# Reordering the first loads of a split-float32 matmul kernel, with one more engine allowed for part of the weights

## The chip, the cores and the metric

The kernel runs on one core of a Trainium2 chip. The metric is device time in microseconds (us). Before the change the median of three runs is 107.62 us (107.62 to 107.70). The core's engines are named as in the profile: PE is TensorE (matmuls; PEld its weight loads), DVE is VectorE, ACT is ScalarE, POOL is GpSimd, SP is SyncE, which here only issues DMAs. A "q" behind a name (SPq, ACTq) is that engine's instruction sequencer, where DMA issues show.

## The reference

With `x` of shape (4, 1024, 512) and one condition vector of 256 elements per batch row:

```python
hidden = concat([cond, cond], -1)                       # (4, 512)
x_mean = mean(x, axis=1, keepdims=True)                 # (4, 1, 512)
fused = concat([x, x_mean * ones, hidden * ones], -1)   # (4, 1024, 1536)
return x + relu(einsum('bld,do->blo', fused, W) + b)    # W: (1536, 512)
```

Everything is float32. `W` has three blocks of 512 rows: the first multiplies `x`, the second the mean, the third the condition. Only the first block needs a large matmul; the other two give one bias vector per batch row.

## The kernel before

**Tiles.** The 4096 rows of `x` are 32 tiles of 128 rows; tile `t` is row `r = t // 8`, `k = t % 8`. A tile needs 128x512 outputs over a contraction of 512, which is cut into J = 4 slices of 128. Each operand is split into a high part rounded to the matmul's float32 format and a low remainder, so that each slice takes three matmuls: high by high, high of x by low of W, low of x by high of W. That makes 12 matmuls with 512 columns per tile.

**Preparing x.** Tiles are grouped in units: tiles 0 and 1 alone, tiles 2-3, 4-5 and 6-7 in pairs, then fours. The first four units (`TURN_PE`) are turned by PE transposes straight from the loaded tile (line 388); later units are loaded a second time in another arrangement (`z`, line 284) and turned on DVE (line 390). A turned piece lies in PSUM, in one of two buffers, or for a few pieces in SBUF. ACT copies it to `hi` (line 415), DVE or POOL subtracts to get `lo` (line 431). For the two single tiles DVE also adds up columns for the mean (`sum`, line 424). A turn may start when the piece two before it has been split (and, for a single tile, added up), because it takes over that buffer.

**Preparing W.** The first block of W comes in two halves of 512 KB, slices 0 and 1 by `load_w(e, 0)`, slices 2 and 3 by `load_w(e, 2)` (line 293). Each slice then has `w_hi` (line 358 on ACT or 359 on DVE) and `w_lo` (line 361, DVE only).

**Finishing.** When a tile's 12 matmuls (line 594) are done, its PSUM bank is read out with or without bias (lines 607, 612), relu follows on ACT (617), `x` is added on POOL (620), and the tile is stored (632). The last four tiles are finished on DVE alone (612, 625), the very last one in two halves. A row's bias comes from the sums, the mean block and the condition block of W and is spread over 128 partitions by two matmuls (line 520).

**The order.** The program fixes, for every engine, one instruction order ahead of time. Each operation is added to a `Plan` with the engines that may run it and their costs, what it depends on, and a due time. `latest_starts` turns due times into latest starts; `simulate` then repeatedly takes the operations that could start first (within 0.1 us of the first on the same engine), gives the turn to the one with the smallest latest start, and puts an operation with several possible engines where it would end first. `run` repeats this 1500 times with random shifts of the latest starts above 12 us and keeps the best order by the planner's own costs. Loads at the head are not planned: the loop at line 296 issues them in the order of its list, and the second entry is the time at which the planner takes them to be there. On the chip the engines keep the planned order and wait on semaphores.

**The head.** SP issues, in this order: tile 0 of x (256 KB), half 0 of W, tile 1 of x, half 1 of W, tiles 2-3 of x, tiles 4-5 of x (512 KB each), then the first slice of the mean block. All go through one DMA queue. PE runs nine warm-up matmuls on a constant (line 235), turns tile 0 (`turn 0`), transposes the condition and runs `N_FILL = 3` more matmuls on ones (`fill`, lines 397 and 401), turns tile 1 (`turn 1`), and starts the products. Products of tiles 0 and 1 are planned matmul by matmul, as `part(t, j, n)`, n = 0 for high by high, 1 for low of W, 2 for low of x. `turn 2` is the first slice of tiles 2-3.

Of the kernel before, what the change touches and what calls it, by code (L numbers as in the profile page):

```python
# [153 lines left out]
def kernel(  # L154
# [22 lines left out]
    nc = tc.nc  # L177
# [12 lines left out]
    N_FIRST = 1  # L190
# [5 lines left out]
    NEVER = 1000.0  # L196
# [3 lines left out]
    KEEP = (0, 1, 2, 3, 4, 8, 9, 10, 16, 17)  # L200
    LO_POOL = {(r, u, j) for r in (1, 2) for u in (0, 1) for j in (1, 3)} | {(0, 4, 3)}

    N_FILL = 3

    const = ctx.enter_context(tc.tile_pool(name="const", bufs=1))
    xpool = ctx.enter_context(tc.tile_pool(name="xpool", bufs=X_BUFS))
# [10 lines left out]
    plan = Plan(["pe", "dve", "act", "pool", "sp", "aq"])  # L217
# [5 lines left out]
    Wv = W.rearrange("(s p j) o -> s p j o", p=P, j=J)  # L223
# [40 lines left out]
    w_x = xpool.tile([P, J, D], F32, tag="x", name="w_x")  # L264
    w_mean = const.tile([P, J, D], F32, name="w_mean")

    def load_x(e, g, i=0, n=G):
        r, k = divmod(g * G, NK)
        if not i:
            xs[g] = xpool.tile([P, G, D], F32, tag="x", name=f"x{g}")  # L270
        e.dma_start(out=xs[g][:, i : i + n], in_=xv[r, :, k + i : k + i + n, :])  # L271
# [17 lines left out]
    SP = 0.72  # L289
    SPZ2 = 1.85  # L290
    SPZ = 1.3
    def load_w(e, j):
        e.dma_start(out=w_x[:, j : j + 2, :], in_=Wv[0, :, j : j + 2])  # L293

    nc.scalar.dma_start(out=c_sb, in_=cond)
    for key, at, e, load in (
        (("x", 0, 0), 4.4, nc.sync, lambda e: load_x(e, 0, 0, 1)),
        (("w", 0), 6.1, nc.sync, lambda e: load_w(e, 0)),
        (("x", 0, 1), 6.8, nc.sync, lambda e: load_x(e, 0, 1, 1)),
        (("w", 2), 8.1, nc.sync, lambda e: load_w(e, 2)),  # L300
        (("x", 0, 2), 9.4, nc.sync, lambda e: load_x(e, 0, 2, 2)),
        (("x", 1, 0), 10.7, nc.sync, lambda e: load_x(e, 1, 0, 2)),
    ):
        load(e)
        plan.done[key] = (at - plan.HANDOVER, 0.0, "sp")
    w_cond = xpool.tile([P, 2, KH, D], F32, tag="x", name="w_cond")

    def load_cond():
        nc.sync.dma_start(
            out=w_cond, in_=W[2 * D : 3 * D].rearrange("(s h p) o -> p s h o", p=P, h=KH)  # L310
        )
# [3 lines left out]
    def load_mean(j, n):  # L315
        nc.sync.dma_start(out=w_mean[:, j : j + n, :], in_=Wv[1, :, j : j + n])

    load_mean(0, N_FIRST) if N_FIRST else None
    plan.free["sp"] = 8.6 + SP * N_FIRST
    plan.add("cond", {"sp": 4 * SP}, [], 13, lambda e: load_cond(), later=2.5)  # L320
    plan.add("w_mean", {"sp": (J - N_FIRST) * SP}, ["cond"], 14,
             lambda e: load_mean(N_FIRST, J - N_FIRST), later=2.5)
# [31 lines left out]
    w_hi = const.tile([P, J, D], F32R, name="w_hi")  # L354
    w_lo = const.tile([P, J, D], F32R, name="w_lo")
    for j in range(J):
        plan.add(("w_hi", j), {"act": 0.62, "dve": 0.45}, [("w", j // 2 * 2)], NEVER, lambda e, j=j: (
            nc.scalar.activation(w_hi[:, j, :], w_x[:, j, :], AF.Copy) if e == "act" else
            nc.vector.tensor_copy(w_hi[:, j, :], w_x[:, j, :])))
        plan.add(("w_lo", j), {"dve": 0.69}, [("w_hi", j)], NEVER,  # L360
                 lambda e, j=j: nc_of[e].tensor_tensor(
                     w_lo[:, j, :], w_x[:, j, :], w_hi[:, j, :].bitcast(F32), ALU.subtract))

# [31 lines left out]
    def fill():  # L395
        for h in range(KH):
            nc.tensor.transpose(
                pw[:, h * B : (h + 1) * B], c_sb[:, h * P : (h + 1) * P], ident[:B, :B]
            )
        for _ in range(N_FILL):  # L400
            nc.tensor.matmul(
                pw[:, KH * B :], lhsT=warm[:, :P], rhs=warm[:, KH * B :], start=True, stop=True
            )

    plan.add(("b",), {"act": 0.25}, [("w_hi", J - 1)], FIRST + 4, lambda e: nc.scalar.dma_start(
        out=b_sb[0:1, :], in_=b.rearrange("(o d) -> o d", o=1)), later=3.0)
    plan.add(("fill",), {"pe": 0.22 * N_FILL + 0.2}, [("turn", 0)], 5.6, lambda e: fill())

    def split_hi(c):
        u, js = pieces[c]  # L410
# [24 lines left out]
    for c, (u, js) in enumerate(pieces):  # L435
        r, k0, n = units[u]
# [11 lines left out]
        w = n * len(js)  # L448
# [273 lines left out]
```

## Time and profile before

| What | Value |
|---|---|
| Median of three runs | 107.62 us |
| The profiled execution | 107.12 us |
| Its span, first to last instruction | 105.3 us |
| PE busy | 100.3 us, 95% of the span |
| DVE / ACT / POOL busy | 78.1 / 58.0 / 73.0 us |
| 512-column product matmuls (line 594) | 372, and 24 with 256 columns |
| Granted PE clock | full in every slice |

A span counts from the first to the last instruction; 1.8 us of the profiled execution lie outside it. Matmuls overlap in the records: one takes about 0.40 us from start to end, while the next starts 0.23 us after it, so that start-to-start times, not durations, say what PE does per matmul. Busy shares are averages; which wait matters is read from the order of events.

### The profile page before, as it was taken

How to read it: one execution, taken by the hardware profiler on the slowest of the kernel's cores; microseconds unless marked ns; L12 is line 12 of the kernel's file. 1: busy time of each engine (PE TensorE's matmuls, PEld its weight loads, DVE VectorE, ACT ScalarE, POOL GpSimd, SP SyncE). 2: the span in 40 equal slices, each digit the busy share in tenths (PEclk: the TensorE clock that was granted, in tenths of full speed). 3: DMA queues.
4: the chain of work that ended last, by engine and by line, in shares of the span. 5: the costliest groups of instructions: out<-in, count | busy, mean ns of one | idle time of the engine just before them, and what ended most of it. 6: DMA issues, size and time to landing. Idle time of an engine off the chain costs nothing.

```text
span 105.3 us, 1466 instructions
## 1 busy us (share of the span) xinstructions
PE 100.3 (95%) x444; PEld 79.1 (75%) x444; DVE 78.1 (74%) x119; ACT 58.0 (55%) x137; POOL 73.0 (69%) x66
## 2 busy tenths in 40 slices
PE   7969999999999999999999999999999999999980
PEld 2446878888878887888788878887888788878870
DVE  0079664769999978699859999798899964295460
ACT  5046566986799770976279773461988122290000
POOL 6000009652999999989959999996899999069200
PEclk9999999999999999999999999999999999999999
DMA  2979999999999999999999999999959755207832
GB/s 71 282 259 380 319 334 297 225 200 197 199 199 199 243 216 353 286 212 265 281 319 388 285 217 341 385 385 346 334 174 348 304 226 218 104 0 275 313 139 70
DMA packets 23905, 26.83 MB, mean 255 GB/s; under 512 B 1237, under 2 KB 14809, under 8 KB 23898
## 3 DMA queue, kind: packets, MB, share of 16 engines
q1 hardware_dynamic: 23888, 26.74, 91.3%
q8 instruction: 3, 0.05, 0.2%
q14 instruction: 4, 0.03, 0.1%
q10 hardware_dynamic: 10, 0.01, 0.0%
HBM read 18.36 MB, written 8.39 MB: 254 GB/s over the span
## 4 chain that ended last, share of the span: by engine, by line
PE 87%; DMA 7%; SPq 2%; DVE 0%; issue 0%
PE po_None L594 81%; DMA x<-in_x_dram 7%; PE po L594 3%; PE xT L388 2%; PE pb L520 2%; SPq L293 1%; SPq L271 1%; DVE o L625 0%; PE po L589 0%
## 5 line engine op out<-in xcount | busy, mean ns | idle before, releaser
L594 PE MATMUL po_None<-w_hi,hi 128*128 128x512 f32 x124 | 49.5, 399 | 0.0
L594 PE MATMUL po_None<-w_hi,lo 128*128 128x512 f32 x124 | 49.5, 399 | 0.0
L594 PE MATMUL po_None<-w_lo,hi 128*128 128x512 f32 x124 | 49.0, 397 | 0.0
L620 POOL TENSOR_TENSOR o<-o,x 128x512 f32<-128x512 f32 x28 | 35.5, 1292 | 4.2 <-ACT o L617 4.1
L390 DVE STREAM_TRANSPOSE xT<-z 128x512 f32<-128x512 f32 (+1 forms) x28 | 28.3, 1040 | 1.6 <-POOL lo L431 1.3
L594 PEld LDWEIGHTS po_None<-w_hi,hi 128*128 128x128 f32 x124 | 23.4, 189 | 5.5 <-ACT hi L415 0.2
L594 PEld LDWEIGHTS po_None<-w_lo,hi 128*128 128x128 f32 x124 | 23.4, 189 | 5.4
L594 PEld LDWEIGHTS po_None<-w_hi,lo 128*128 128x128 f32 x124 | 23.4, 189 | 5.4
L415 ACT ACTIVATE hi<-xT 128x512 fp32r<-128x512 f32 (+1 forms) x38 | 20.2, 534 | 10.1 <-PE xT L388 7.1
L431 DVE TENSOR_TENSOR lo<-xT,hi 128x512 fp32r<-128x512 f32 (+1 forms) x29 | 16.8, 581 | 8.9 <-ACT hi L415 8.6
L617 ACT ACTIVATE o<-o 128x512 f32<-128x512 f32 x28 | 16.6, 626 | 5.0 <-DVE o L612 2.7
L612 DVE TENSOR_TENSOR o<-po_None,bias 128x512 f32<-128x512 f32 x18 | 11.6, 680 | 6.7 <-issue 3.4
L612 POOL TENSOR_TENSOR o<-o,bias 128x512 f32<-128x512 f32 x10 | 13.0, 1306 | 2.6 <-issue 1.3
L495 DVE SCALAR_TENSOR_TENSOR acc<-w_mean,tot,acc 128x512 f32<-128x512 f32 x15 | 11.2, 749 | 1.3 <-ACT acc L489 0.9
L478 POOL TENSOR_TENSOR wc<-w_cond 128x512 f32<-128x512 f32 x2 | 2.5, 1294 | 13.6 <-DMA w_cond<-in_L_cond_W_dram 13.6
L431 POOL TENSOR_TENSOR lo<-xT,hi 128x512 fp32r<-128x512 f32 (+1 forms) x9 | 11.2, 1239 | 0.9 <-ACT hi L415 0.9
L607 ACT ACTIVATE o<-po_None 128x512 f32<-128x512 f32 x10 | 5.8, 592 | 7.8 <-PE po_None L594 7.8
L415 ACT ACTIVATION_READ_ACCUMULATOR hi<-xT 128x1 f32 x36 | 7.0, 195 | 0.0
L506 POOL TENSOR_TENSOR cond<-bL,term 128x512 f32<-128x512 f32 x4 | 5.2, 1304 | 2.1 <-ACT term L501 2.1
L388 PEld LDWEIGHTS xT<-ident,x 128*128 128x128 f32 x24 | 4.2, 203 | 3.3 <-DMA x<-in_x_dram 1.4
L526 ACT ACTIVATE bias<-pb 128x512 f32<-128x512 f32 x4 | 2.4, 598 | 7.7 <-PE pb L520 7.7
L501 ACT ACTIVATE term<-wc,cT 128x512 f32<-128x512 f32 x8 | 5.6, 722 | 1.0 <-POOL cond L506 1.0
(51 smaller groups left out, 58.1 us busy)
## 6 DMA issues: line engine op xcount, KB each, us to landing
out_dram<-o SPq DMA_DIRECT2D x31, 256.0 KB, 3.6
z<-in_x_dram SPq DMA_DIRECT2D x24, 256.0 KB, 8.2
x<-in_x_dram SPq DMA_DIRECT2D x6, 1024.0 KB, 8.4
x<-in_x_dram SPq DMA_DIRECT2D x3, 512.0 KB, 8.3
w_x<-in_L_cond_W_dram SPq DMA_DIRECT2D x2, 512.0 KB, 5.8
w_cond<-in_L_cond_W_dram SPq DMA_DIRECT2D x1, 1024.0 KB, 9.5
w_mean<-in_L_cond_W_dram SPq DMA_DIRECT2D x1, 768.0 KB, 9.0
x<-in_x_dram SPq DMA_DIRECT2D x2, 256.0 KB, 4.1
```

The lines of the kernel that those rows point to most:

```text
L388: nc.tensor.transpose(v[:, (m * n + i) * P : (m * n + i + 1) * P], x_t[:, j], ident)
L390: nc.vector.transpose(v[:, : n * P].rearrange("p (n t) -> p n t", t=Q), zs[u].rearrange("p n (a j) -> p n j a", j=J)[:, : n * NQ, js[0], :],)
L415: nc.scalar.activation(hi[c][:, :m], xT[c][:, :m], AF.Copy, accum_out=sums[:, r, js[0], s : s + 1] if len(js) == 1 else None,)
L431: nc_of[e].tensor_tensor(lo[c][:, :m], xT[c][:, :m], hi[c][:, :m].bitcast(F32), ALU.subtract)
L495: nc.vector.scalar_tensor_tensor(acc[r], w_mean[:, j, :], totals[r][:, j : j + 1], acc[r], ALU.mult, ALU.add)
L501: nc.scalar.activation(terms[r, k], wc[:, k], AF.Copy, scale=cT[:, k, r : r + 1])
L506: nc.gpsimd.tensor_tensor(conds[r], conds[r] if k else bL, terms[r, k], ALU.add)
L594: nc.tensor.matmul(pos[key][:, :w], lhsT=v[p][:, c], rhs=m[:, j, d], start=(not h and todo[key] == 3 * J), stop=(todo[key] == 1),)
L607: nc.scalar.activation(o_tile(t), pos[t], AF.Copy)
L612: nc_of[e].tensor_tensor(v if t >= ALONE else o_tile(t), v, biases[t // NK][:, d], ALU.add)
L617: nc.scalar.activation(outs[t], outs[t], AF.Relu)
L620: nc.gpsimd.tensor_tensor(outs[t], outs[t], x_tile(t), ALU.add)
```

## The change

Tile 1 of x is issued right behind tile 0, ahead of both halves of W; W's halves and the rest keep their order. The times that the planner assumes for the head's loads are changed with it. `fill` now follows `turn 1` instead of `turn 0` and has four matmuls on ones instead of three. `w_lo` may be planned on POOL as well as on DVE. `load_w` gets the number of slices as an argument; both calls still load two. The planner's SP is free 0.3 us later. The whole order is searched anew with these inputs.

```diff
-    N_FILL = 3
+    N_FILL = 4
...
-    def load_w(e, j):
-        e.dma_start(out=w_x[:, j : j + 2, :], in_=Wv[0, :, j : j + 2])
+    def load_w(e, j, n):
+        e.dma_start(out=w_x[:, j : j + n, :], in_=Wv[0, :, j : j + n])
...
         (("x", 0, 0), 4.4, nc.sync, lambda e: load_x(e, 0, 0, 1)),
-        (("w", 0), 6.1, nc.sync, lambda e: load_w(e, 0)),
-        (("x", 0, 1), 6.8, nc.sync, lambda e: load_x(e, 0, 1, 1)),
-        (("w", 2), 8.1, nc.sync, lambda e: load_w(e, 2)),
-        (("x", 0, 2), 9.4, nc.sync, lambda e: load_x(e, 0, 2, 2)),
-        (("x", 1, 0), 10.7, nc.sync, lambda e: load_x(e, 1, 0, 2)),
+        (("x", 0, 1), 5.0, nc.sync, lambda e: load_x(e, 0, 1, 1)),
+        (("w", 0), 6.7, nc.sync, lambda e: load_w(e, 0, 2)),
+        (("w", 2), 8.3, nc.sync, lambda e: load_w(e, 2, 2)),
+        (("x", 0, 2), 9.6, nc.sync, lambda e: load_x(e, 0, 2, 2)),
+        (("x", 1, 0), 10.9, nc.sync, lambda e: load_x(e, 1, 0, 2)),
...
-    plan.free["sp"] = 8.6 + SP * N_FIRST
+    plan.free["sp"] = 8.9 + SP * N_FIRST
...
-        plan.add(("w_hi", j), {"act": 0.62, "dve": 0.45}, [("w", j // 2 * 2)], NEVER, lambda e, j=j: (
+        plan.add(("w_hi", j), {"act": 0.62, "dve": 0.45}, [("w", {0: 0, 1: 0, 2: 2, 3: 2}[j])], NEVER, lambda e, j=j: (
...
-        plan.add(("w_lo", j), {"dve": 0.69}, [("w_hi", j)], NEVER,
+        plan.add(("w_lo", j), {"dve": 0.69, "pool": 1.33}, [("w_hi", j)], NEVER,
...
-    plan.add(("fill",), {"pe": 0.22 * N_FILL + 0.2}, [("turn", 0)], 5.6, lambda e: fill())
+    plan.add(("fill",), {"pe": 0.22 * N_FILL + 0.2}, [("turn", 1)], 5.8, lambda e: fill())
```

## The prediction

> **What bounds the kernel now.** I read the chain that ended last first, in order of time.
>
> ```profile
> 1.63 0.42 SPq L271
> 2.10 0.43 SPq L293
> 2.53 0.04 issue
> 2.57 7.38 DMA x<-in_x_dram
> 9.95 0.14 issue
> 10.09 0.48 PE xT L388 x2
> 10.57 0.94 PE po_None L594 x4
> ```
>
> Up to 9.95 us the end is set by one transfer, tiles 2-3 of x, issued at 2.57 and landed at 9.95; from turn 2 at 10.09 it is PE to the end. The busy times of the stretches 7 to 10.09, 10.09 to 102.25 and 102.25 to the end (columns: length, then PE, PEld, DVE, ACT, POOL, clock, DMA share, GB/s) say how firm that is:
>
> ```profile
> 7.00:10.09 3.09, 2.85 (x13) 2.03 (x14) 2.94 (x5) 1.75 (x3) 0.00 (x0) 1.00 0.97 360
> 10.09:102.25 92.16, 92.15 (x413) 74.81 (x413) 73.50 (x110) 53.50 (x130) 71.36 (x57) 1.00 0.95 262
> 102.25:105.30 3.05, 0.00 (x0) 0.00 (x0) 0.42 (x1) 0.00 (x0) 0.00 (x0) 1.00 0.26 89
> ```
>
> PE is busy 92.15 of 92.16 us behind turn 2, at full clock. The change removes no matmul, so time can only be won ahead of 10.09, or by having more of PE's work done by then. Last, the PE timeline of the head:
>
> ```profile
> 4.51 0.63 PE L388 MATMUL xT<-ident,x 128*128 128x128 f32 x4
> 5.28 0.82 PE L401 MATMUL pw<-const-bfloat16-1.0 128*128 128x504 bf16 x3
> 6.98 0.75 PE L388 MATMUL xT<-ident,x 128*128 128x128 f32 x4 [0.89 <-DMA x<-in_x_dram]
> 7.49 0.48 PE L594 MATMUL po_None<-w_hi,hi 128*128 128x512 f32 x1
> ...
> 9.45 0.40 PE L594 MATMUL po_None<-w_hi,lo 128*128 128x512 f32 x1
> 10.09 0.48 PE L388 MATMUL xT<-ident,x 128*128 128x128 f32 x2 [0.24 <-DMA x<-in_x_dram]
> ```
>
> Turn 1 waits for tile 1 until 6.98, then nine products run (7.49 to the slot that ends at 9.68), then PE waits for tiles 2-3. The question is therefore: how many products stand ahead of turn 2 after the change, when are they done, and when do tiles 2-3 land?
>
> **Part 1, the loads.** x1 is issued at about 1.16 instead of 1.63, half 0 of W at 1.6 instead of 1.16. Landings of half 0 and half 1, and what started on half 0:
>
> ```profile
> DMA to landing us min/median/max: 5.1/5.8/6.5
> 6.29 0.63 ACT L358 ACTIVATE w_hi<-w_x 128x512 fp32r<-128x512 f32 x1 [0.52 <-DMA w_x<-in_L_cond_W_dram]
> ```
>
> So half 0 landed at 1.16 + 5.1 = 6.26, half 1 at 2.10 + 6.5 = 8.6; tile 0 at 0.73 + 2.9 = 3.6 (the shortest landing of x). The trace shows the landings in the order of issue. Half 0 in third place has the same 1,024 KB up to its end as x1 had, so I put it where x1 was: 6.93, 0.05 before turn 1 started. Bounds from the two W rows: 5.1 us from its new issue gives 6.7, 6.5 us gives 8.1; the equal bytes decide for 6.93. x1, between 3.6 and 6.26, I put at 4.9, halfway for half the bytes. Half 1 and tiles 2-3 keep place, issue and bytes ahead: 8.6 and 9.95. Behind them SP's next issues wait for landings (w_cond started at 6.29, when half 0 landed, a z load at 6.95, when x1 did); these two waits now hang on x1 and on half 0, at 4.9 and 6.93. w_cond can be issued over 1 us earlier, but stands behind the same transfers in the queue, and its reader on POOL started only at 15.84. Cost nothing, gain nothing.
>
> **Part 2, turn 1 and fill.** PE runs turn 0 from 4.51 to 5.07, turn 1 (0.47 = 7.45 - 6.98) to 5.54, the two condition transposes (5.28 - 5.07 = 0.21), then four matmuls on ones at some 0.21 each: done at 6.6. What hides this is the wait for W. Without that cover, if x1 landed after about 6.1, turn 1 and fill (1.5 us together) would stand ahead of the first product. 0.47 us of transposes leave the stretch behind 6.98.
>
> **Part 3, splitting.** ACT: hi of tile 0 at 5.17, of tile 1 next, 0.60 each, done by 6.4; w_hi of slice 0 from 6.98 to 7.61 (0.63 of line 358). DVE: lo of tile 0 from 5.80, lo of tile 1 from 6.40 to 7.09 (back to back they start 0.60 apart: 9.01, 9.61, 10.21), then w_hi of slice 1 at 7.00 to 7.50 (0.42), w_lo of slice 0 from 7.64 to 8.33, both sums to 9.5, w_lo of slice 2 to 10.2. Following the planner's rule by hand with its new costs, two of the four w_lo, of slices 1 and 3, end first on POOL. (The same walk through the old inputs gives exactly the old trace's order of DVE and of the nine products; I use it for order alone.) POOL has no instruction between 2.3 and 15.84, and takes 1.30 for such a subtraction (line 431, 128x512, on POOL):
>
> ```profile
> L431 POOL TENSOR_TENSOR lo<-xT,hi 128x512 fp32r<-128x512 f32 x8 | 10.4, 1302 | 0.0
> L361 DVE TENSOR_TENSOR w_lo<-w_x,w_hi 128x512 fp32r<-128x512 f32 x4 | 2.7, 684 | 0.1
> ```
>
> So w_lo of slice 1 runs from 7.55 to 8.85, of slice 3 from about 9.85 to 11.15. DVE loses 2 x 0.68 of work in a stretch where nothing waits for it. The Trainium skill, "GPSIMD Engine Reference", section 1, warns that GpSimd shares its SBUF interfaces with VectorE and contends with VectorE instructions that have two SBUF inputs; w_lo of slice 0 on DVE is one, beside w_lo of slice 1 on POOL, and the trace of before has no such pair. If POOL stood still for that one, by the page slice 1 would come 0.68 later, at 9.53, just when it is needed below, and the sum would stay the same.
>
> **Part 4, the products.** The walk gives for PE: high by high and low of x for slice 0 of tiles 0 and 1 (four that need w_hi only), high by high of slice 1, the two with w_lo of slice 0, low of x of slice 1, and the one with w_lo of slice 1. Then turn 2. Again nine. First at 7.66 (w_hi 7.61 plus the 0.05 that PEld took behind hi at 8.37 to 8.42), then 0.234 apart: the sixth at 8.83 needs w_lo of 8.33, the ninth at 9.53 that of 8.85, and the slot ends at 9.77. Turn 2 also needs the first sum, done by 8.9. So PE comes to turn 2 at 9.77 and waits for tiles 2-3: 10.09 as before. The idle of 0.4 ahead of turn 2 becomes 0.3, the gain of 0.47 from turn 1 is eaten by the 0.17 later first product and by that wait.
>
> **Sum.** At 10.09 both orders have done both turns, fill and nine products; 15 parts of tiles 0 and 1 and all else are left, 92.16 us. Loads: 0. Fill's fourth matmul: 0 (under the wait for W). POOL: 0. Turn 2: 10.09 - 10.09 = 0. Span 105.3, its execution 107.12 with the 1.8 around it; the median of the runs shown stands 0.5 above that, and I add the same nothing to it: 107.62, rounded to **107.6 us**. A kernel like this can be told from no change by about 0.2%, 0.2 us.
>
> **Rivals.** (a) Faster: PE's slack of 0.32 at turn 2 turns into time. For it: if tiles 2-3 land earlier, PE follows down to 9.77, and if the order puts a tenth product ahead of turn 2, that fits too (0.23). The queue ran unevenly: 232 GB/s between 4 and 7 us against 360 from 7 to 10.09, so the order may ease that. Against: bytes ahead of tiles 2-3 are the same. Time 107.62 - 0.3 = 107.3; with half 0 at 6.7 as well, 0.55, 107.07.
> (b) Slower: half 0 of W is late. Place: the first product, which now hangs on the third load alone. It decides from 6.93 + 0.32 = 7.25 on; past that, each us is paid. At the upper bound of 8.1 PE comes to turn 2 at 9.77 + 1.17 = 10.94: 0.85 later, 108.5; with 7.7, 108.1. For it: W's rows spread from 5.1 to 6.5. Against: equal bytes.
> (c) Slower: the re-searched order, from 15 us on, lets PE wait once for a split piece. Price: one hi of 0.60 on ACT, as when a lo waits for its hi; 108.2, less if some of it was covered. For it: 92 us without a gap leave no way to improve, only to lose. Against: DVE at 74 of 92 us, POOL at 71, ACT at 54 have room.
> (d) The planner doesn't use POOL: then w_lo of slices 1 and 3 come later on DVE (9.7 and 11.5 or so), one other part takes the ninth place, and the time stays 107.6; this counts within the forecast.
>
> **How the numbers follow.** No change 0.40 (107.6, its own range 107.4 to 107.8), (a) 0.24, (b) 0.18, (c) 0.18. Faster 0.24, same 0.40, slower 0.36. The range reaches to 107.2 at the fast side (0.4 of the 0.55 that (a) could give) and to 108.4 at the slow one, just under the bound of (b); about 2 in 10 lie outside.
>
> **What would show it.** In the new profile: turn 1 behind turn 0 at about 5.1 and the first product near 7.7 (parts 1 to 3); two subtractions of line 361 on POOL; nine products, then a wait for x ahead of the third turn at 10.1 (part 4); PE busy without a gap from there to 102.25. I am wrong if tiles 2-3 land far from 9.95, if PE comes to turn 2 after them, if more than nine products stand ahead of it, or if PE waits after 15 us.

## The result, and the profile after

| | Before | After |
|---|---|---|
| Median (six runs each, side by side) | 107.66 us | 109.37 us |
| Lowest to highest | 107.62 to 109.29 | 108.28 to 111.27 |
| Ratio, 95% interval | | 1.0133 (1.0086 to 1.0180) |
| Profiled execution, span | 107.12, 105.3 us | 108.28, 106.5 us |
| End of the last product | 102.25 us | 103.43 us |

The change makes the kernel 1.3% slower; 107.6 was forecast. The ratios here leave out runs more than 1.5% above the fastest of their kernel, so they are not quite the quotients of the medians. The profiled execution of after is the quickest of its six, so what its trace shows is the smaller part of the loss.

The chain that ended last, in order of time (start, length, what), is no longer DMA up to turn 2 and PE from there:

```profile
1.64 5.72 DMA w_x<-in_L_cond_W_dram
7.37 0.02 issue
7.39 0.64 ACT w_hi L358
8.03 0.02 issue
8.05 1.69 DVE w_lo L361
9.74 0.60 DVE sums L424
10.34 1.22 DVE w_hi L359
11.56 0.61 DVE sums L424
12.18 0.14 issue
12.31 0.48 PE xT L388 x2
```

Half 0 of W, issued at 1.64, lands at 7.36; from there the chain goes through the splitting of W on DVE, and PE sets the end only from 12.31, 2.2 us later than before. In the chain two DVE steps stand out: a `w_lo` of 1.69 and a `w_hi` of 1.22, where the rows of before have 0.68 and 0.42. The timelines of DVE and POOL beside each other (start, length, engine, line, operation; in brackets the idle time ahead and what ended it):

```profile
7.39 0.43 DVE L359 CAST w_hi<-w_x 128x512 fp32r<-128x512 f32 x1 [0.81 <-DMA w_x<-in_L_cond_W_dram]
8.05 1.69 DVE L361 TENSOR_TENSOR w_lo<-w_x,w_hi 128x512 fp32r<-128x512 f32 x1 [0.23 <-ACT w_hi L358]
9.66 0.68 DVE L424 TENSOR_REDUCE sums<-xT 128x4 f32<-128x512 f32 x1
10.27 1.30 DVE L359 CAST w_hi<-w_x 128x512 fp32r<-128x512 f32 x1
```

```profile
7.90 1.29 POOL L361 TENSOR_TENSOR w_lo<-w_x,w_hi 128x512 fp32r<-128x512 f32 x1 [5.63 <-DVE w_hi L359]
9.99 1.29 POOL L361 TENSOR_TENSOR w_lo<-w_x,w_hi 128x512 fp32r<-128x512 f32 x1 [0.80 <-ACT w_hi L358]
```

Each long DVE instruction lies beside one of POOL's two and ends 0.3 to 0.55 us behind it (9.74 against 9.19, 11.57 against 11.28). The sum at 9.66, which reads a turned piece in PSUM, has its usual 0.68, though half of it lies beside POOL's second subtraction. On PE:

```profile
3.99 1.11 PE L388 MATMUL xT<-ident,x 128*128 128x128 f32 x8
...
5.25 1.03 PE L401 MATMUL pw<-const-bfloat16-1.0 128*128 128x504 bf16 x4
8.07 0.50 PE L594 MATMUL po_None<-w_hi,hi 128*128 128x512 f32 x1 [1.79 <-ACT w_hi L358]
...
9.11 0.40 PE L594 MATMUL po_None<-w_hi,hi 128*128 128x512 f32 x1
9.79 0.74 PE L594 MATMUL po_None<-w_lo,hi 128*128 128x512 f32 x2 [0.29 <-DVE w_lo L361]
...
10.84 0.39 PE L388 MATMUL xT<-ident,x 128*128 128x128 f32 x2
...
12.31 0.48 PE L388 MATMUL xT<-ident,x 128*128 128x128 f32 x2 [0.38 <-DVE sums L424]
```

Both turns run back to back and fill behind them, then PE waits for half 0, once more for the long `w_lo`, and once for the second sum, which stands behind the long cast on DVE. The stretches up to, and behind, that last wait (length, then PE, PEld, DVE, ACT, POOL busy, clock, DMA share, GB/s):

```profile
8.07:12.31 4.24, 3.57 (x14) 2.33 (x15) 4.24 (x5) 1.11 (x3) 2.41 (x2) 1.00 1.05 340
12.31:103.43 91.12, 91.10 (x408) 74.01 (x408) 72.31 (x108) 53.46 (x128) 71.40 (x57) 1.00 0.95 258
```

Behind 12.31 PE has no gap, as before. So all of the loss of this execution lies in the head. A load is counted complete when all of 16 engines have reported; the table has the first, eighth and last of these 16 events, in us, with the loads in the order of issue:

| Before | issue | 1st, 8th, last | After | issue | 1st, 8th, last |
|---|---|---|---|---|---|
| tile 0 | 0.73 | 3.08, 3.23, 3.60 | tile 0 | 0.73 | 3.17, 3.25, 3.50 |
| half 0 | 1.16 | 4.52, 4.68, 6.27 | tile 1 | 1.18 | 3.83, 3.93, 4.04 |
| tile 1 | 1.63 | 5.17, 5.53, 6.94 | half 0 | 1.64 | 5.33, 6.79, 7.36 |
| half 1 | 2.10 | 7.78, 8.24, 8.61 | half 1 | 2.11 | 7.31, 8.69, 9.26 |
| tiles 2-3 | 2.57 | 9.46, 9.67, 9.95 | tiles 2-3 | 2.58 | 9.04, 10.05, 10.58 |

Although the first three loads hold 1,024 KB in both orders, they end at 7.36 instead of 6.94, and what stands behind them is 0.6 later too.

### The profile page after: what moved, and what is told of

It reads as the page before. It is cut to its first block, busy times and chain, and to the rows that moved or that the text cites. A ratio compares the mean times of both kernels' runs of the same rounds, so it can differ in the third digit from the quotient of the medians.

```text
span 106.5 us, 1467 instructions
## 1 busy us (share of the span) xinstructions
PE 100.2 (94%) x445; PEld 79.1 (74%) x445; DVE 78.9 (74%) x118; ACT 57.8 (54%) x136; POOL 75.6 (71%) x68
## 4 chain that ended last, share of the span: by engine, by line
PE 86%; DMA 5%; DVE 4%; SPq 1%; ACT 1%; issue 0%
PE po_None L594 79%; DMA w_x<-in_L_cond_W_dram 5%; PE po L594 3%; PE pb L520 2%; PE xT L388 2%; DVE w_lo L361 2%; DVE w_hi L359 1%; DVE sums L424 1%; SPq L271 1%; ACT w_hi L358 1%; DVE o L625 0%; PE po L589 0%
## 5 line engine op out<-in xcount | busy, mean ns | idle before, releaser
L361 POOL TENSOR_TENSOR w_lo<-w_x,w_hi 128x512 fp32r<-128x512 f32 x2 | 2.6, 1290 | 6.4 <-DVE w_hi L359 5.6
```

The source lines that it names most:

```text
L361: lambda e, j=j: nc_of[e].tensor_tensor(w_lo[:, j, :], w_x[:, j, :], w_hi[:, j, :].bitcast(F32), ALU.subtract))
```

## The experiments

Two suspects stand in the profile: the order of the loads, and POOL beside DVE. Each kernel was timed against the kernel before on the same chip; ratios have 95% intervals. "Lands" is the last of the 16 events in the kernel's profiled execution.

**1. The two parts taken apart.** First the change without POOL:

```diff
-        plan.add(("w_lo", j), {"dve": 0.69, "pool": 1.33}, [("w_hi", j)], NEVER,
+        plan.add(("w_lo", j), {"dve": 0.69}, [("w_hi", j)], NEVER,
```

> The changed kernel, but w_lo can run on VectorE alone, as before; the new order of the loads and the four matmuls on ones stay. Theory P (GpSimd's w_lo and VectorE's instructions with two SBUF inputs, or the fast cast, hold each other up): no VectorE instruction of lines 359 and 361 takes over 0.70 us (1.69 and 1.30 in the changed kernel), PE is not held by w_lo or by the sums, and the profiled span falls from 106.5 to about 105.9 or less. Theory L (the new order of loads alone makes it slow, because half 0 of W and tiles 2-3 land 0.4 and 0.6 us later): the w_lo wait on PE goes but turn 2 still starts near 10.7, and the span stays 0.6 above that of the kernel before, 105.9. If L were all, 106.4.

Measured: 110.0 us (108.9 to 112.23), ratio 1.0145 (1.0075 to 1.0215). The long DVE instructions are gone, yet half 0 lands still later, 8.71, and PE waits longer for it. DVE and PE of this kernel:

```profile
8.74 0.43 DVE L359 CAST w_hi<-w_x 128x512 fp32r<-128x512 f32 x1 [1.99 <-DMA w_x<-in_L_cond_W_dram]
9.40 0.69 DVE L361 TENSOR_TENSOR w_lo<-w_x,w_hi 128x512 fp32r<-128x512 f32 x1 [0.23 <-ACT w_hi L358]
```

```profile
9.42 0.50 PE L594 MATMUL po_None<-w_hi,hi 128*128 128x512 f32 x1 [2.97 <-ACT w_hi L358]
```

Both theories had put this span at 106.4 us or less; it is 108.5. So the change without POOL is enough for the loss, and taking POOL away gives nothing back in these runs. The other way round, the old loads with POOL allowed (the same line edited in the kernel before):

> The kernel before with one thing of the change: w_lo may run on GpSimd. Loads, fill and all else as before; two of the four w_lo go to GpSimd. Theory P: of lines 359 and 361 on VectorE one or two instructions take 1.2 to 1.7 us, VectorE's sums come 1 to 2 us later, turn 2 or turn 3 waits for a sum, and the time is 0.4 to 1.2 us above before. Theory L: half 0 lands at 6.3 and tiles 2-3 at 9.95, and the time is that of before within 0.2.

Measured: 108.32 us (107.71 to 109.38), 1.0044 (1.0004 to 1.0084). Half 0 lands at 6.02, tiles 2-3 at 10.04, as before the change. One `w_lo` on DVE takes 1.44, one on POOL 1.66:

```profile
7.10 0.69 DVE L361 TENSOR_TENSOR w_lo<-w_x,w_hi 128x512 fp32r<-128x512 f32 x1
9.83 1.44 DVE L361 TENSOR_TENSOR w_lo<-w_x,w_hi 128x512 fp32r<-128x512 f32 x1
```

```profile
7.27 1.66 POOL L361 TENSOR_TENSOR w_lo<-w_x,w_hi 128x512 fp32r<-128x512 f32 x1 [5.00 <-DVE w_hi L359]
9.44 1.28 POOL L361 TENSOR_TENSOR w_lo<-w_x,w_hi 128x512 fp32r<-128x512 f32 x1 [0.51 <-ACT w_hi L358]
```

The price of POOL in the old order, searched anew with it, is about 0.4%, barely clear of none.

Third, nothing of the change, but POOL, idle at that time, is given four subtractions on the landed half 0, whose output nobody reads:

```diff
+    spare = const.tile([P, D], F32, name="spare")
+    for _ in range(4):
+        nc.gpsimd.tensor_tensor(spare, w_x[:, 0, :], w_x[:, 1, :], ALU.subtract)
```

> The kernel before with its own order, and four extra subtractions on GpSimd that read half 0 of W and write a scratch tile, from about 6.3 to 11.5 us, while GpSimd was idle before. Nothing waits for them. Theory P: w_hi and w_lo on VectorE beside them take 1.2 us or more each (0.42 and 0.68 before), while lo (one input in PSUM) and the sums keep 0.68; PE waits for w_lo and the time rises by 1 us or more. Rival: GpSimd slows nothing, and the time is that of before within 0.2.

Measured: 108.09 us (107.82 to 109.08), 1.0044 (1.0005 to 1.0084). DVE, and POOL's four in one line (line numbers are three higher here):

```profile
5.87 1.36 DVE L362 CAST w_hi<-w_x 128x512 fp32r<-128x512 f32 x1
7.16 1.77 DVE L364 TENSOR_TENSOR w_lo<-w_x,w_hi 128x512 fp32r<-128x512 f32 x1
8.85 0.68 DVE L427 TENSOR_REDUCE sums<-xT 128x4 f32<-128x512 f32 x1
9.45 0.68 DVE L434 TENSOR_TENSOR lo<-xT,hi 128x512 fp32r<-128x512 f32 x1
10.05 0.68 DVE L364 TENSOR_TENSOR w_lo<-w_x,w_hi 128x512 fp32r<-128x512 f32 x1
...
11.25 1.18 DVE L364 TENSOR_TENSOR w_lo<-w_x,w_hi 128x512 fp32r<-128x512 f32 x1
```

```profile
5.68 6.19 POOL L321 TENSOR_TENSOR spare<-w_x 128x512 f32<-128x512 f32 x4 [3.41 <-DMA w_x<-in_L_cond_W_dram]
```

The cast (0.42 alone) and two of the `w_lo` (0.68 alone), with SBUF inputs, are held; the sum and `lo`, which read a turned piece in PSUM, are not. The `w_lo` at 10.05 is not held either: POOL's fourth subtraction starts behind it, at 10.15, and takes 1.73 instead of 1.30. So it is the one that starts later that is held, as in the rows of the old loads above, where POOL started 0.17 behind DVE's 7.10 and took 1.66, and DVE started 0.39 behind POOL's 9.44 and took 1.44. In all the pairs of these traces and of the changed kernel's two that overlap by more than 0.03 us, the later one ends a fixed time behind the end of the earlier: `w_lo` on DVE 0.54 to 0.55, a cast 0.29, POOL's subtraction 1.14 to 1.16, each some 0.14 less than its length alone. That the two hold each other is shown without any of the change. The time rose by 0.4% only, where 1 us or more had been expected.

Last, the changed kernel once more, on the same chip:

> The changed kernel unchanged, for a second look at its loads and at the spread of its times (108.3 to 109.8 so far). If the late loads belong to the order: half 0 of W lands at 7.2 or later again and tiles 2-3 at 10.4 or later. If they were chance: near 6.9 and 9.95. The long VectorE instructions of lines 359 and 361 come again either way.

Measured: 109.2 us (108.65 to 110.36), 1.0117 (1.0062 to 1.0171); half 0 at 8.14, tiles 2-3 at 10.78. The loss repeats; the landing at 7.36 was an early one.

**2. Why is half 0 late? What stands behind it.** Perhaps half 1, right behind half 0 now, reads the same memory and hinders it. In the first experiment's kernel tiles 2-3 were put between them:

```diff
-        (("w", 2), 8.3, nc.sync, lambda e: load_w(e, 2, 2)),
-        (("x", 0, 2), 9.6, nc.sync, lambda e: load_x(e, 0, 2, 2)),
+        (("x", 0, 2), 8.0, nc.sync, lambda e: load_x(e, 0, 2, 2)),
+        (("w", 2), 9.6, nc.sync, lambda e: load_w(e, 2, 2)),
```

> As e1 (new order of the head's loads, w_lo on VectorE alone), but tiles 2-3 of x stand between the two halves of W: tile 0, tile 1, half 0, tiles 2-3, half 1. So far half 0 landed at 7.4, 8.7 and 8.1 in third place (three traces) and at 6.3, 6.0 and 5.6 in second, where tile 1 lies between the halves. Theory N (half 1 right behind half 0 reads the same stretch of memory and holds half 0 up): half 0 lands at 7.0 or earlier and the first product starts by 7.8. Theory B (half 0 is late because of the place and the bytes ahead alone): it lands at 7.4 to 8.7 again. The time itself may rise, since half 1 comes 1.3 us later.

Measured: 110.32 us (109.17 to 112.22), 1.0192 (1.0135 to 1.0249); half 0 lands at 8.59. And in the kernel before, half 1 was moved up to stand right behind half 0:

```diff
-        (("x", 0, 1), 6.8, nc.sync, lambda e: load_x(e, 0, 1, 1)),
-        (("w", 2), 8.1, nc.sync, lambda e: load_w(e, 2)),
+        (("w", 2), 7.4, nc.sync, lambda e: load_w(e, 2)),
+        (("x", 0, 1), 8.1, nc.sync, lambda e: load_x(e, 0, 1, 1)),
```

> The kernel before with tile 1 of x behind both halves of W: tile 0, half 0, half 1, tile 1. Half 0 keeps second place. Theory N: with half 1 right behind it, half 0 lands 1 us later than in the kernel before, at 7.0 or later. Theory B: it lands at 5.6 to 6.3 as before. The time is not what is asked: tile 1 comes at about 8.6, and PE may wait for it.

Measured: 107.18 us (106.41 to 108.83), 0.9953 (0.9905 to 1.0001); half 0, second in the queue, lands at 5.81. Half 0 is late with half 1 apart, and early with half 1 close behind: this theory falls.

**3. The clock.** In the first experiment's profile the granted clock drops behind the wait. If that drop made the time, ten more matmuls on ones under the wait should keep it off (`N_FILL = 14` in that kernel).

> As e1, but 14 matmuls on ones instead of four, so that PE has work up to about 8.3. Theory C (the clock granted to PE falls when it waits some 3 us for half 0, as in e1, where one slice shows half the clock and the mean is 0.984): the clock stays at 1.00 whenever half 0 lands late, and the median falls from e1's 110.0 to about 109.2. Rival: the clock plays no part; the median stays at 109.5 to 110.3. If half 0 lands as early as 7.4, the long fill costs 0.2.

Measured: 110.88 us (109.63 to 111.69), 1.0244 (1.0179 to 1.0309). The clock stays at full speed and no time comes back: half 0 lands at 8.28, the first product starts at 9.27, and the new order waits 0.6 us for a `lo`. The loss does not need the drop: the changed kernel, too, took 108.34 and 109.4 in two executions at full clock. That the drop is free is not shown.

**4. Place or bytes.** Half 0 as two loads of one slice, first in the old order with tile 1 between them, so that the first slice needs fewer bytes ahead:

```diff
-        (("w", 0), 6.1, nc.sync, lambda e: load_w(e, 0)),
-        (("x", 0, 1), 6.8, nc.sync, lambda e: load_x(e, 0, 1, 1)),
+        (("w", 0), 5.2, nc.sync, lambda e: load_w(e, 0, 1)),
+        (("x", 0, 1), 5.9, nc.sync, lambda e: load_x(e, 0, 1, 1)),
+        (("w", 1), 6.8, nc.sync, lambda e: load_w(e, 1, 1)),
```

> The kernel before with half 0 of W as two loads of one slice each, in the order tile 0, slice 0, tile 1, slice 1, half 1, tiles 2-3. If the first product hangs on the first bytes of W, slice 0 lands by about 5.0, PE's first product starts at about 6.5 instead of 7.5, more than nine products stand ahead of turn 2, and the time falls by up to 0.9 to about 106.8. Rival: W's first reads are slow in any order and cut; slice 0 or tile 1 lands at 6.3 or later, and the time is 107.4 to 108.

Measured: 108.99 us (107.39 to 110.16), 1.0048 (1.0010 to 1.0086). The ten runs fall on two levels, five up to 108.63 and five from 109.35; the ratio is that of the lower one. Slice 0 lands at 5.59, slice 1 at 7.38; the profiled execution is the quickest. This brings no gain.

Then tiles 2-3 of x took half 0's third place in the first experiment's kernel, both halves of W behind them, in a single execution:

```diff
-        (("w", 0), 6.7, nc.sync, lambda e: load_w(e, 0, 2)),
...
+        (("x", 0, 2), 6.7, nc.sync, lambda e: load_x(e, 0, 2, 2)),
+        (("w", 0), 8.3, nc.sync, lambda e: load_w(e, 0, 2)),
```

> As e1, but tiles 2-3 of x (512 KB, as much as half 0) take third place, and both halves of W come behind: tile 0, tile 1, tiles 2-3, half 0, half 1. Theory W (it is W's first reads): tiles 2-3 land by 6.0, 1.4 us behind tile 1, the rate seen for x elsewhere, and half 0 is slow in fourth place, landing 3 us or more behind them. Rival (third place itself, or what the queue can supply, is the limit): tiles 2-3 land at 7.4 to 8.7 like half 0 did.

Measured: 110.11 us. Tiles 2-3, third now, report first at 5.37, eighth at 5.66, and last at 8.58. The landing is late, as with W in that place, but by one engine: the other fifteen had reported by 6.60.

Next, W's half 0 as two slices in third and fourth place, the rest as in the first experiment (five loads ahead of tiles 2-3):

```diff
-        (("w", 0), 6.7, nc.sync, lambda e: load_w(e, 0, 2)),
+        (("w", 0), 5.9, nc.sync, lambda e: load_w(e, 0, 1)),
+        (("w", 1), 6.7, nc.sync, lambda e: load_w(e, 1, 1)),
```

> As e1, but half 0 comes as two loads of one slice (packets of 2 KB instead of 4): tile 0, tile 1, slice 0, slice 1, half 1, tiles 2-3. If packets of 4 KB make half 0 late, slice 0 lands by 5.5, slice 1 by 6.6, and the time falls to that of the kernel before. If W's first reads are slow whatever their size, slice 0 lands at 6.5 or later, slice 1 at 7.4 or later, and the time is 0.5 to 1.5% above before.

Measured: 106.64 us (105.86 to 107.69), 0.9870 (0.9824 to 0.9916): faster than the kernel before. Slice 0 lands at 6.83, slice 1 at 7.50. The same kernel again, in another series with more runs:

> The same kernel as g3 (tile 0, tile 1, slice 0, slice 1, half 1, tiles 2-3; w_lo on VectorE alone), measured again in more rounds, since it came out 1.3% under the kernel before. If that holds: 106.0 to 106.9, slice 0 landed by 6.9 and the first product by 7.5, more than nine products ahead of turn 2. If it was one lucky series: 107.2 or more.

Measured: 107.25 us (106.72 to 108.64), 1.0000 (0.9960 to 1.0039). The gain did not repeat; that slices take away the loss of the new order did (slice 0 at 6.42, slice 1 at 7.07). It is not the number of loads by itself, then: half 1 and tiles 2-3 have one load more ahead of them here, and land at 8.57 and 9.90, as before the change (8.61 and 9.95).

The decisive pair changes the number of loads ahead of half 0 and leaves the bytes nearly as they were. In the first experiment's kernel tiles 0 and 1 come as one load of 512 KB, so that half 0 is second with the same bytes ahead as in the changed kernel:

```diff
-        (("x", 0, 0), 4.4, nc.sync, lambda e: load_x(e, 0, 0, 1)),
-        (("x", 0, 1), 5.0, nc.sync, lambda e: load_x(e, 0, 1, 1)),
+        (("x", 0, 0), 5.0, nc.sync, lambda e: load_x(e, 0, 0, 2)),
+        (("x", 0, 1), 5.0, nc.sync, lambda e: None),
```

> As e1, but tiles 0 and 1 come in one load of 512 KB, so that half 0 of W is the second load and is issued at about 1.25 us instead of 1.64; the bytes ahead of it are the same. If the place or the time of issue makes half 0 late (the engines starve from 3.5 to 5 us because the third load's packets reach them late): half 0 lands by 7.1 and 14 or more of the engines have a packet under way from 3.5 to 5. If the 512 KB of x ahead make it late: it lands at 7.4 to 8.7 again and the same dip shows. The time: turn 0 starts some 0.4 later; 108 to 108.8 in the first case, 109 to 110 in the second.

Measured: 108.17 us (106.81 to 110.97), 1.0038 (0.9994 to 1.0082). Half 0 lands at 6.78, half 1 at 8.09, tiles 2-3 at 9.44; the first product starts at 7.49, exactly as before the change, and turn 2 at 9.93. The head's loss is gone; what keeps this kernel from being quicker is a later wait of PE, 1.0 us for `acc_lo` (line 514), at the end of a chain over the loads of `w_cond` and of a `z`. Whether the new order or these loads brought it is open.

And the opposite: the kernel before with one small load, 64 KB, between tile 0 and half 0, so that half 0 is third with only 320 KB ahead of it:

```diff
+    def load_w_behind(e):
+        e.dma_start(out=spare, in_=xv[B - 1, :, NK - 1, :P])
+        load_w(e, 0)
...
-        (("w", 0), 6.1, nc.sync, lambda e: load_w(e, 0)),
+        (("w", 0), 6.1, nc.sync, lambda e: load_w_behind(e)),
```

> The kernel before with one more load between tile 0 and half 0 of W: 64 KB (512 bytes per partition of x, into a scratch tile that nothing reads). Half 0 becomes the third load, is issued at about 1.6 us instead of 1.16, and has 64 KB more ahead, worth about 0.2 us. If the place in the queue and the later issue make the third load late: half 0 lands at 7 or later (6.0 on average in second place), a dip of engines without a packet shows, and the time rises by 0.5 us or more. If the bytes did it: it lands at 5.8 to 6.5 and the time stays within 0.3 of before.

Measured: 109.46 us (108.64 to 111.09), 1.0119 (1.0043 to 1.0195); half 0 lands at 8.31 instead of 6.27, tile 1 at 8.99 instead of 6.94. PE of this kernel (line numbers six higher):

```profile
4.50 0.76 PE L394 MATMUL xT<-ident,x 128*128 128x128 f32 x4
...
9.04 1.13 PE L394 MATMUL xT<-ident,x 128*128 128x128 f32 x4 [2.81 <-DMA x<-in_x_dram]
```

In this execution 64 KB cost 2 us of landing. It is the slowest of the kernel's four (111.09 us), so 2 us is not the typical price; the loss, of the size of the change's, stands on the other three, 108.64 to 109.96. The stretch of the transfers from 3.5 to 6 us in four kernels (columns as above; the DMA share and GB/s at the end are what counts). Before the change:

```profile
3.50:6.00 2.50, 2.50 (x12) 1.22 (x10) 0.20 (x1) 0.60 (x1) 0.00 (x0) 1.00 0.99 208
```

Tiles 0 and 1 in one load:

```profile
3.50:6.00 2.50, 2.50 (x11) 1.83 (x9) 0.00 (x0) 0.40 (x1) 0.00 (x0) 1.00 1.03 274
```

The changed kernel:

```profile
3.50:6.00 2.50, 2.50 (x17) 1.72 (x15) 0.71 (x2) 1.08 (x2) 0.00 (x0) 1.00 0.77 176
```

The small load between:

```profile
3.50:6.00 2.50, 2.50 (x12) 1.35 (x10) 0.07 (x1) 0.60 (x1) 0.00 (x0) 1.00 0.64 159
```

With half 0 second, the 16 DMA engines have packets all the time here (0.99 and 1.03); with half 0 third, they stand partly idle although the loads have been issued (0.77 and 0.64). Idle engines are not all of it: over the runs on one queue the busy share is 0.86 to 1.03 with half 0 second, and 0.61 to 0.87 with half 0 or tiles 2-3 third; at 0.86 half 0 landed once at 5.61 and once at 8.59, and with slice 0 second and early (5.59) the share was 0.70. The other part is seen in the 16 events of half 0, from the trace's DMA completions, in us:

```
before            4.52 4.53 4.56 4.58 4.59 4.60 4.64 4.68 5.69 5.99 6.00 6.06 6.18 6.21 6.22 6.27
tiles in one      5.72 5.79 5.80 5.82 5.85 5.88 5.89 5.95 5.98 6.01 6.13 6.27 6.29 6.31 6.62 6.78
after             5.33 6.00 6.21 6.23 6.28 6.33 6.77 6.79 6.82 6.86 6.89 6.93 6.95 7.14 7.20 7.36
without POOL      5.30 5.36 5.46 6.38 6.39 6.40 6.43 6.45 7.08 7.16 7.26 7.29 7.50 7.62 7.63 8.71
small load        4.92 5.04 5.09 5.22 6.34 6.42 6.43 6.53 6.57 6.69 6.71 6.80 6.85 6.87 7.29 8.31
```

In third place the typical engine is late here, and in two of the three rows a single engine comes a full us behind the fifteenth.

**5. Ways around it.** Half 0 issued by ACT instead, on its own queue, so that tile 1 is second on SP's (from the first experiment's kernel):

```diff
+    load_w(nc.scalar, 0, 2)
...
-        (("w", 0), 6.7, nc.sync, lambda e: load_w(e, 0, 2)),
```

> As e1, but half 0 of W is issued by ScalarE, on its own queue, at about 0.9 us, while SyncE issues tile 0, tile 1, half 1. Same bytes in all. Theory S (in third place of one queue, half 0's packets come to the DMA engines late: between 3.5 and 6 us only 6 to 12 of 16 engines had a packet under way): half 0 lands at 6.5 or earlier, tile 1 at 5.5 or earlier, the first product starts by 7.2, and the time is that of the kernel before or up to 0.6 less, 107.0 to 107.6. Theory W (the first reads of W are slow wherever they stand): half 0 lands at 7.4 to 8.7 and the time stays 1 to 2% above before.

Measured: 109.25 us (107.27 to 109.64), 0.9997 (0.9951 to 1.0043); the runs fall on two levels, four from 107.27 to 108.14 and eight from 109.15 on, and the ratio is that of the four. In the profiled execution, one of the quick ones, half 0 lands before 5.95 and tiles 2-3 at 9.25, but tile 1 only at 6.60, and fill, now behind turn 1, stands ahead of the first product at 8.22. With fill put back behind turn 0, and three matmuls on ones as in the kernel before:

> As g1 (half 0 of W on ScalarE's queue, tile 1 behind tile 0 on SyncE's), with fill behind turn 0 and three matmuls on ones, as in the kernel before. In g1 half 0 landed before 5.95, tile 1 at 6.6, tiles 2-3 at 9.25, but fill stood behind turn 1 and put the first product to 8.22. If fill alone ate the gain: the first product starts by 7.3, and the time falls to 106.6 to 107.1, in most runs. If the two queues are unsteady, half or more of the runs stay at 109 as in g1.

Measured: 108.32 us (106.62 to 108.94), 1.0020 (0.9971 to 1.0069). The condition, which is issued on ACT as well, lands late, and fill waits 0.69 us for it; the turn at 15.56 waits 1.3 us for a `lo`. The ratio is that of the quickest five of twelve runs; the version is not better than before.

Last, one load for both tiles, slices for half 0, and a short fill (`N_FILL = 2`):

> What the cause suggests for a faster kernel: tiles 0 and 1 in one load, then slice 0, slice 1 and half 1 of W, then tiles 2-3; two matmuls on ones behind turn 1; w_lo on VectorE alone. Slice 0 is the second load and should land by 5.8, slice 1 by 6.7, tiles 2-3 by 9.6, as in h3; the first product starts by 6.9, twelve or more products stand ahead of turn 2, and the time is 106.0 to 106.9. If the slices bring the late landing back (slice 1 and half 1 are third and fourth): slice 1 at 7.5 or later and 107.2 to 108.

Measured: 110.54 us (109.17 to 112.01), 1.0185 (1.0113 to 1.0257), where 106.0 to 106.9 had been expected. The loads come as wanted (slice 0 at 5.59, slice 1 at 7.23, tiles 2-3 at 9.89), and the first product starts at 6.46, 1.0 us ahead of the kernel before. What PE waited for in this kernel (total, times, longest; line numbers one higher):

```profile
PE xT L389 <- DVE lo L432: 1.0, 1, 1.0
PE po_None L595 <- DVE lo L432: 0.9, 1, 0.9
...
PE xT L389 <- DMA x<-in_x_dram: 0.7, 1, 0.7
```

The early products run into the wait for tiles 2-3, and PE waits 1.9 us for `lo` pieces, one of the two waits behind a `z` load in the chain that ended last; how much of that the order searched anew made is open. A head that is 1 us earlier brought nothing here.

No version beat the kernel before for certain; the nearest are half 1 right behind half 0, 0.9953 (0.9905 to 1.0001), and the slices in third place, 0.9870 once and 1.0000 the second time.

## Why the prediction was wrong, step by step

**What held.** Tile 1 landed at 4.04, earlier than my 4.9. Turn 1 ran right behind turn 0, and fill was hidden under the wait for W (1.79 us were left of it). Two of the four `w_lo` went to POOL, those of slices 1 and 3; nine products stand ahead of turn 2; PE runs without a gap behind the head (91.10 of 91.12 us), so rival (c) did not come in the changed kernel. Late waits did come in experiments: 0.6 us in the kernel with the long fill, 1.0 us in the one with both tiles in one load, 1.9 us in the last one.

**The step that failed: part 1, half 0 at 6.93.** "Half 0 in third place has the same 1,024 KB up to its end as x1 had, so I put it where x1 was." It landed at 7.36 in the profiled execution and at 8.14 in the repeated one. Equal bytes were not the measure, and rival (b) came true, which I had given 0.18. The landings by the runs:

| Half 0, its place | kernel | ahead | eighth event | lands |
|---|---|---|---|---|
| second | before | 256 KB | 4.68 | 6.27 |
| second | halves together | 256 KB | 5.22 | 5.81 |
| second | POOL, old loads | 256 KB | 5.09 | 6.02 |
| second | idle POOL busy | 256 KB | 5.09 | 5.61 |
| second | tiles in one | 512 KB | 5.95 | 6.78 |
| third | after; again | 512 KB | 6.79; 6.21 | 7.36; 8.14 |
| third | without POOL | 512 KB | 6.45 | 8.71 |
| third | halves apart | 512 KB | 6.49 | 8.59 |
| third | long fill | 512 KB | 5.96 | 8.28 |
| third | small load between | 320 KB | 6.53 | 8.31 |

The bytes that I argued with are right for the second place: 512 KB ahead and 512 KB of its own end at 6.78, where I had said 6.93. In the third place 320 KB ahead were, in the one execution seen, as late as 512. The last event tells the places apart in every row; the eighth does not at equal bytes (5.95 second, 5.96 to 6.79 third). A sign stood in the trace of before: tile 1, third there, had its eighth event at 5.53 and its ninth at 6.48, and half 0 ahead of it 4.68 and 5.69. Half of the engines were a us late in both, so tile 1's landing, which I used as the measure of 1,024 KB, was not set by bytes alone, and engines can lose that us in second place too. The price of (b) had a limit of its own, 8.1 for the landing, taken from half 1's row; 8.14 and 8.71 were beyond it. For the 7.36 of the profiled execution (b) gives 0.11 us only; it had left tiles 2-3 at 9.95.

What is shown is that one more load ahead, of almost no bytes, is enough for the loss. Not shown is why: a third load is also one issued at 1.63 or later, and no run separates the place from the moment. The size of the packets is a further rival: half 0 comes in packets of 4 KB, its slices, which cost nothing in third and fourth place, in packets of 2 KB, and no run changes that size alone. Nor is it known why the engines stand idle, or why the last of them reports 0.6 to 2.9 us behind the eighth. That stays open.

**Terms that followed from it.** Half 1 and tiles 2-3 "keep place, issue and bytes ahead: 8.6 and 9.95" fell with it: 9.26 and 10.58, since they stand behind half 0.

**The second step: part 3, w_lo of slice 0 at its usual 0.68.** The Trainium skill, "GPSIMD Engine Reference", section 8, says that GpSimd contends with VectorE instructions that have two SBUF inputs or a 2-port mode. I had let POOL stand still for it and had priced that at nothing. The traces show that the one that starts later is held. In the changed kernel that was DVE both times, by 1.69 - 0.68 = 1.0 us for `w_lo` (8.05, behind POOL's 7.90) and by 1.30 - 0.42 = 0.9 us for the cast, which has one SBUF input (10.27, behind POOL's 9.99). My own times had POOL first too, 7.55 against 7.64, so by this rule the price fell on DVE. POOL, where it starts later, is held by up to 1.73 - 1.30 = 0.43. My walk through the planner had also put the cast of slice 2 on ACT; the planner chose DVE and set it ahead of the second sum, beside POOL's second subtraction, so the sum that turn 3 needs came at the end of the longer chain.

**The sum, mended for the profiled execution.** First product 8.07 instead of 7.66: 0.41, the late half 0. Nine products in 2.77 us (8.07 to 10.84) instead of 2.11 (7.66 to 9.77): 0.66, of which 0.45 is the slot that waits for `w_lo` (9.79 less 9.11 + 0.23). PE so comes to turn 2 1.07 later than forecast; the slack of 0.32 that I had counted covers some of it, and 0.75 is left (10.84 less 10.09). Tiles 2-3, landed at 10.58, would by themselves have given 10.72: the two delays overlap, and products in time would alone have won 0.1. Behind turn 2 another 0.43 goes (103.43 - 10.84 = 92.59 against 92.16): the wait of turn 3 for the second sum. Together 1.18, the difference of the two ends of PE's work.

The median lies another 1.09 above this execution. In the repeated run's trace, 0.4 us longer in span, half 0 is 0.78 later; that the spread of the runs comes from this landing fits, but landings are known only for profiled executions.

**The two causes don't add.** POOL cost 0.4% in the old order. In the new one the kernel without POOL is not faster (1.0145 beside 1.0133 and 1.0117). The load order alone brings a loss of this size; how much POOL adds to it the runs don't tell, since the landing of half 0 differs by more than a us between profiled executions (7.36, 8.14, 8.71), and two of the three runs behind 1.0145 had a mean clock of 0.984, where those of the changed kernel behind 1.0133 had 0.997 to 1.

## What to carry to other kernels

When loads are reordered at a kernel's start, a load's place in the queue can cost by itself, beside the bytes ahead: look at when the typical and when the last of the DMA engines reports, not only at the landing, and move a load that the first product hangs on later in the queue only with slack for the worst landing, not the median one. An idle engine is not free capacity: price the pair of instructions that will lie beside each other, and ask which starts first, before work is moved to it. And when the whole order is searched anew, a head that is quicker by 1 us may be given back later; look for waits past the head in every variant.

## What the runs showed of the hardware that was not expected

**The third load.** With half 0 of W in third place the DMA engines were busy for 0.77 (after) and 0.64 (small load between) of the stretch from 3.5 to 6 us, though over 1.5 MB had been asked for by 3.1 us. Part of the delay lies in single packets: of half 0's 4 KB packets, 0.16 us at the median, eleven took over 0.7 us (up to 1.3) after the change. But nine did before it, with a landing at 6.27, three in the repetition with one at 8.14, and none with both tiles in one load. A late engine can carry its delay through the loads behind: in the run with tiles 2-3 third, the last event came 2.9 us behind the eighth (8.58 and 5.66), and the next two loads show 1.7 and 2.4.

**POOL and DVE.** Of a POOL subtraction and a DVE subtraction or cast, all 128x512 with SBUF inputs only, the one that started later waited for the other: DVE's subtraction took 1.18 to 1.77 us instead of 0.68, its cast 0.91 (in the repetition) to 1.36 instead of 0.42, POOL's up to 1.73 instead of 1.30. The one that started first kept its length. DVE instructions that read PSUM kept their 0.68.

**The clock.** Waits of PE of 2 to 3 us can cost clock as well. The page's row of the granted clock in the first experiment's kernel (waited 2.97 us) and in the one with the small load between (2.81 us), in slices of 2.7 us:

```profile
PEclk9999599999999999999999999999999999999999
```

```profile
PEclk9995579999999999999999999999999999999999
```

The mean clock is 0.984 and 0.969. A wait of 2.0 us gave 0.984 with the halves apart, one of 2.08 us full clock in the repetition of the changed kernel. The Trainium skill, "TensorE: Matmul & The Clock Gate", part 1, tells of a free-running window of about 3.4 us, after which an idle PE falls to half clock; the half clock agrees, and waits shorter than that window, 2.0 to 2.97 us, were enough here.
